# Moving a block's state stores, its last degree sums and its first late masks between nodes of a graph recurrence

## Chip, core and metric

One core of a Trainium2 chip runs the whole program: four graph layers over 64 graphs of 256 nodes with 256 features, in float32. The metric is device time in microseconds (us) of one execution, lower is better. The kernel is written for the five engines of the core: TensorE (PE, matrix products), VectorE (DVE), ScalarE (ACT), GpSimd (POOL) and SyncE (SP, which here only issues DMAs).

## What is computed

Layer 0 is a recurrence over the 256 nodes of a graph: node i's parent vector is the sum of the states of the other nodes weighted by column i of the adjacency, divided by row i's degree; a gated cell makes the new state of node i from it, and later nodes see that new state. All 64 graphs advance together. Layers 1 to 3 (a normalized graph convolution and two attention layers) follow, each with residual and layer norm; the change doesn't touch them.

```python
d = jnp.sum(adj, axis=-1)
dinv = jnp.where(d != 0, 1.0 / jnp.where(d != 0, d, 1.0), 0.0)
norm_adjT = jnp.swapaxes(adj, 1, 2) * dinv[:, :, None]

def step(h, i):
    x = jnp.take(h_e, i, axis=1)
    row = jnp.take(norm_adjT, i, axis=1)
    x_par = jnp.einsum('bj,bjd->bd', row, h)
    iou = x @ W_ioux.T + b_ioux + x_par @ W_iouh.T + b_iouh
    r, z = jnp.split(iou, 2, axis=1)
    r, z = (jax.nn.sigmoid(r), jax.nn.sigmoid(z))
    hc = jnp.tanh(x @ W_coux.T + b_coux + x_par * r @ W_couh.T + b_couh)
    h_new = z * x_par + (1.0 - z) * hc
    h = jax.lax.dynamic_update_slice(h, h_new[:, None, :], (0, i, 0))
    return (h, None)
h_out, _ = jax.lax.scan(step, h_e, jnp.arange(n))
```

## The kernel before

`_recurrence` walks the nodes one at a time (the loop at line 768). Nodes are counted in blocks of T = 32 (block k, node i inside it) and in octets of U = 8 (p = n % 8). The loop is traced under a manual schedule, so every engine works its instructions strictly in the order in which the code states them; SP's one queue carries nearly all DMAs, in the order of the code too.

A node's chain is short and serial: transpose of the parent vector (`flip`, 618), products with the gate weights (`h_part`, 611), a sigmoid on ACT (835), transpose (837), the product `rT` on DVE (839), products again, tanh on ACT (872), and on DVE `zcc` (874) and the next parent vector `xp` (877). The rest of the node's work is laid beside this chain:

- A state's share in later sums. DVE pushes a new state into the sums of the near nodes (`push`, 636), POOL into the farther ones of the octet and the next (`push_far`, 674 and 678). POOL also makes `ready` (816), the finished sum of the next node times its inverse degree; DVE reads it at 864.
- The late side, for states that are up to some 48 nodes old. They lie in `Hw`, a ring of 64 rows a half of the graphs (partition = 64 x half + node % 64); `into_ring` (667) writes each new state there with two DMAs, in the nodes with p of 4 to 7. In the nodes with p of 0 to 3, PE multiplies ring rows by `An`, the masked adjacency of the block (527). The results are copied to `lb`, sent to DRAM (`Lb<-lb`, 507) and read back in another layout (`late_sb<-Lb`, 513) about a node later. POOL adds `late_sb` to the sums (887) at p = 6 and 7, that is at nodes 14, 15, 22, 23 and so on of the block, before any node of the next octet.
- The early side, for older states. They are stored in DRAM (`Hd`) by `flush` (646), read back by `early_load`, multiplied on PE (424), and come to POOL as `early_sb` (829) at p = 3 and 4.
- Tables of the next block, made during this one. `degrees` (292) is a generator of 14 steps. Four times it loads four rows of adjacency a graph at a time (`rows`, one buffer, two DMAs of 256 KB) and sums them on DVE in two halves (304); then it inverts the sums and copies the result into `dinv`. The loop takes a step of it at the nodes of a list (911). `late_load` (460) queues loads of `raw`, the adjacency that `An` is cut from, and POOL multiplies it with the window mask in four pieces (`cut`, 485) at fixed nodes. The first piece also forces any load of `raw` that is still in the list of waiting loads.

`flush` copies 16 ring rows of both halves with two DMAs. A row of the ring is 32 KB on one partition, so a DMA moves 512 KB from 16 neighbouring partitions (480 KB where 15 rows are stored). At i = 16 a block stores 31 rows: the second half of the block before, and the first half of its own but for the newest state, which `state_out` (652) stores straight from its tile.

Within a node, the order on SP is: ring writes, loads from the list (p < 4), steps placed by `at_step`, the reads for the next octets, the stores of `flush`, then a step of `degrees`.

Of the kernel before, what the change touches and what calls it, by code (L numbers as in the profile page):

```python
# [70 lines left out]
def _recurrence(tc, ident, Hd, x, adj, W_ioux, b_ioux, W_iouh, b_iouh, W_coux, b_coux, W_couh, b_couh, wide, then):  # L71
# [21 lines left out]
    T = 32  # L93
# [7 lines left out]
    HB = B // 2  # L101
    FAR = (2, 4, 4, 4, 4, 4, 3, 4)

    with ExitStack() as ctx:
# [14 lines left out]
        def ring(lo, hi):  # L119

            while lo < hi:
                end = min(hi, (lo // W + 1) * W)
                yield lo, end, lo % W
                lo = end
# [125 lines left out]
        def next_load(n):  # L250
            if loads:
                loads.pop(0)[1](n)
# [10 lines left out]
        def load_later(out, in_, rank):  # L263

            begun = []

            def f(n):
                with nc.allow_non_contiguous_dma(reason="bias vector across partitions"):
                    nc.sync.dma_start(out, in_)
                begun.append(n)  # L270

            loads.append((rank, f))
            loads.sort(key=lambda e: e[0])
            return begun
# [5 lines left out]
        def at_step(n, f):  # L280
            transfers.setdefault(n, []).append(f)
# [10 lines left out]
        def degrees(k):  # L292

            R = 4
            HT = T // 2
            deg = work.tile([P, HT], F32, tag="deg", name=f"deg_{k}")
            for r in range(0, HT, R):
                rows = stream.tile([P, R, N], F32, tag="rows", name=f"rows_{k}_{r}", bufs=1)
                for h in range(2):
                    at = k * T + h * HT + r  # L300
                    nc.sync.dma_start(rows[h * B:(h + 1) * B], adj[:, at:at + R, :])
                yield
                for e in range(0, R, 2):
                    nc.vector.tensor_reduce(
                        deg[:, r + e:r + e + 2], rows[:, e:e + 2, :], AX.X, ALU.add
                    )
                    yield
            zero = work.tile([P, HT], F32, tag="deg0", name=f"deg0_{k}")
            inverse(deg, zero)
            yield  # L310
            dinv_from(deg, k)
# [148 lines left out]
        def late_load(k, n=None):  # L460


            An = blk.tile([P, HB, U, T // U], F32, tag="An", name=f"An_{k}")
            raw = stream.tile([P, HB, T], F32, tag="raw", name=f"raw_{k}", bufs=1)
            first, last = k * T - W + T // 2, k * T + T // 2
            if first < 0:
                nc.gpsimd.memset(raw, 0.0)
            begun = []
            for lo, hi, at in ring(max(first, 0), last):
                for g in range(2):  # L470
                    to = raw[g * W + at:g * W + at + hi - lo]
                    of = adj[g * HB:(g + 1) * HB, lo:hi, k * T:(k + 1) * T].rearrange(
                        "b j i -> j b i"
                    )
                    if n is None:
                        nc.scalar.dma_start(to, of)
                    else:
                        begun.append(load_later(to, of, 1.5))

            def cut(lo):  # L480
                while not all(begun):
                    next_load(now)
                part = raw[:, lo:lo + HB // 4].rearrange("p b (s u) -> p b s u", u=U)
                take = window[k % 2].rearrange("p (s u) -> p s u", u=U).unsqueeze(1)
                nc.gpsimd.tensor_mul(
                    An[:, lo:lo + HB // 4].rearrange("p b u s -> p b s u"), part,
                    take.to_broadcast(list(part.shape)),
                )

            for e in range(4):  # L490
                if n is None:
                    cut(e * HB // 4)
                else:
                    at_step(n + (12, 15, 20, 23)[e], lambda e=e: cut(e * HB // 4))
            return An

        def late(first):
# [43 lines left out]
        def load_S(k, n=None):  # L541

            S = blk.tile([P, LAG + T, T], F32, tag="S", name=f"S_{k}")
            lag = min(LAG, k * T)
            to, of = S[0:B, LAG - lag:], adj[:, k * T - lag:(k + 1) * T, k * T:(k + 1) * T]
            begun = [0] if n is None else load_later(to, of, 1.5)
            if n is None:
                nc.sync.dma_start(to, of)
            if not lag:
                nc.gpsimd.memset(S[:, LAG - 1], 0.0)  # L550

            def double():
                while not begun:
                    next_load(now)
                nc.sync.dma_start(S[B:, LAG - lag:], S[0:B, LAG - lag:])

            return S, double

        def chain_S(k):

            Sd = blk.tile([P, T], F32, tag="Sd", name=f"Sd_{k}")
            flat = tables[k]["S"].rearrange("p j i -> p (j i)")
            first = (LAG - 1) * T
            nc.vector.tensor_mul(
                Sd, flat[:, first:first + (T - 1) * (T + 1) + 1:T + 1],
                dinv[:, k * T:(k + 1) * T],
            )
            return Sd

        def load_x(a):  # L570

            xq = stream.tile([P, U // 2, D], F32, tag="xq", name=f"xq_{a}")
            for h in range(2):
                at = a * U + h * U // 2
                nc.sync.dma_start(xq[h * B:(h + 1) * B], x[:, at:at + U // 2, :])
            return xq
# [63 lines left out]
        def flush(lo, hi):  # L640

            for lo in range(max(lo, 0), hi, T // 2):
                end = min(hi, lo + T // 2)
                for g in range(2):
                    at = g * W + lo % W
                    nc.sync.dma_start(
                        Hd[lo:end, g * HB:(g + 1) * HB, :], Hw[at:at + end - lo]
                    )

        def state_out(n, hs):  # L650
            for o in range(2):
                nc.sync.dma_start(Hd[n][:, o * P:(o + 1) * P], hs[o * B:(o + 1) * B])
# [72 lines left out]

        tables[0]["Sd"] = chain_S(0)
        tables[0]["An"] = late_load(0)
        xq = {a: load_x(a) for a in range(2)}
        for a in range(3):
# [38 lines left out]
        for now in range(N):  # L768
            n = now
            k, i = divmod(n, T)  # L770
# [124 lines left out]
                sums_in(n // U + 3)  # L895
            if p == 2 and n // U + 2 < N // U:
                xq[n // U + 2] = load_x(n // U + 2)
            if i == T // 2:
                state_out(n - 1, hs)
                flush(n - T, n - 1)  # L900
            if n == N - U + 3:
                assert all(j >= N - U for j, _ in ring_in)
                flush(N - T // 2, N - U)
# [4 lines left out]
            if k + 1 < NB:  # L908
                if i == 0:
                    background = degrees(k + 1)  # L910
                if i in (0, 2, 3, 8, 10, 11, 12, 15, 16, 17, 19, 20, 22, 24):
                    next(background, None)
                if i == 0:
                    tables[k + 1]["S"], double = load_S(k + 1, n)
                    at_step(n + 19, double)
                    tables[k + 1]["An"] = late_load(k + 1, n)
                if i == 28:
                    tables[k + 1]["Sd"] = chain_S(k + 1)
# [554 lines left out]
def kernel(ctx: ExitStack, tc: tile.TileContext, ins, out):  # L1473
# [14 lines left out]
    def load_layers(load):  # L1488
        weights.extend(
            _load_layers(nc, wide, load, ins["L1_gnn_W"], ins["L1_gnn_b"], l2, l3)  # L1490
        )

    _recurrence(
        tc, ident, Hd, x, adj,
        *(ins["L0_gnn_" + n] for n in (
# [44 lines left out]
```

## Time and profile before

| what | us |
|---|---|
| time, median of 3 runs (lowest, highest) | 3335.34 (3333.89, 3336.39) |
| the profiled execution: time, span of its instructions | 3328.66, 3326.6 |
| the recurrence, node 0's `rT` to node 255's | 139.9 to 1486.5 |
| `L304`, sums of degree rows on DVE, 56 of them, each | 0.68 |
| `L485`, mask pieces on POOL, 32 of them, each | 0.74 |
| `L887`, adds of the late side on POOL, 60 of them, each | 1.27 |

Every node has one `rT` product (L839), so in the timeline of DVE the starts of L839 divide the recurrence into nodes. The interval called 19 runs from node 19's `rT` to node 20's, and holds the end of node 19, where the side work of that node stands. Some of them, in us:

| block | 10 | 11 | 13 | 16 | 18 | 19 | 20 | 21 | 22 | 23 |
|---|---|---|---|---|---|---|---|---|---|---|
| 0 | 5.0 | 5.2 | 4.8 | 5.7 | 6.0 | 5.2 | 4.8 | 4.5 | 4.9 | 8.1 |
| 1 | 5.0 | 5.2 | 4.8 | 5.6 | 4.8 | 14.6 | 6.9 | 4.5 | 5.5 | 12.7 |
| 2 | 5.0 | 5.2 | 4.8 | 5.4 | 4.8 | 12.0 | 7.2 | 4.5 | 4.5 | 4.4 |
| 3 | 5.0 | 5.2 | 4.6 | 9.9 | 4.8 | 10.5 | 6.8 | 4.6 | 4.6 | 4.5 |
| 4 | 5.0 | 5.1 | 7.9 | 11.0 | 4.8 | 11.5 | 7.7 | 4.6 | 4.6 | 4.5 |
| 5 | 5.0 | 5.1 | 4.4 | 6.0 | 5.9 | 8.4 | 6.0 | 4.5 | 4.8 | 4.4 |
| 6 | 5.0 | 5.2 | 4.4 | 6.1 | 4.8 | 8.7 | 6.7 | 4.4 | 4.4 | 4.6 |
| 7 | 4.8 | 4.8 | 4.7 | 5.6 | 4.8 | 4.8 | 4.4 | 4.4 | 4.4 | 4.4 |

Block 0 has nothing to store from a block before it, and block 7 has no next block whose degrees it would sum.

### The profile page before, as it was taken

What the parts mean: (1) busy time and instruction counts of PE and PEld (TensorE: products, weight loads), DVE (VectorE), ACT (ScalarE), POOL (GpSimd) and SP (SyncE); (2) the same over time, 40 slices, a digit from 0 to 9 for tenths busy, and PEclk for the clock granted to TensorE, in tenths of its full rate; (3) what the DMA queues carried; (4) which work ended last, traced back from release to release, by engine and by line L of the source; (5) the groups of instructions that cost most, each with busy time, mean ns of one, the idle gap of its engine ahead of it and who ended that gap; (6) DMA issues with size and microseconds to landing.
All of it is one profiled execution on the core that took longest, in us unless ns stands there. A gap on an engine that the chain in (4) does not pass through costs nothing.

```text
span 3326.6 us, 80047 instructions
## 1 busy us (share of the span) xinstructions
PE 3083.6 (93%) x28332; PEld 2279.5 (69%) x28332; DVE 2625.7 (79%) x7511; ACT 1834.3 (55%) x4690; POOL 1924.5 (58%) x2230
## 2 busy tenths in 40 slices
PE   5799979898989898986999999999999999999997
PEld 4565646565555555554888888888888888888885
DVE  3476757787767787864888888888888888888886
ACT  0154535454545454543666666666666666666664
POOL 2376757776767788853555555555555555555543
PEclk8899989999999999997999999999999999999998
DMA  9864556686866675334233333333333333333310
GB/s 293 249 169 126 156 149 157 167 186 165 199 169 159 160 175 151 103 73 99 61 77 77 77 77 77 79 79 77 82 79 80 77 79 77 78 80 78 77 45 20
DMA packets 806730, 385.73 MB, mean 116 GB/s; under 512 B 525260, under 2 KB 774232, under 8 KB 802648
## 3 DMA queue, kind: packets, MB, share of 16 engines
q1 hardware_dynamic: 788632, 363.66, 45.2%
q10 hardware_dynamic: 17696, 16.91, 1.5%
q8 instruction: 227, 3.72, 0.5%
q14 instruction: 175, 1.43, 0.1%
HBM read 261.75 MB, written 99.61 MB: 109 GB/s over the span
## 4 chain that ended last, share of the span: by engine, by line
PE 79%; DVE 8%; DMA 7%; issue 2%; ACT 1%; SPq 1%; POOL 1%; DVEq 0%; ACTq 0%; POOLq 0%
PE mm L1017 14%; PE rc L611 7%; PE rc L603 4%; PE s L1243 4%; PE mm_3v L1017 4%; PE mm_2f L1017 4%; PE mm_2v L1017 3%; PE mm_3f L1017 3%; PE mm_t L1017 3%; PE late L527 3%; PE mm_g L1017 3%; PE mm_2w L1017 3%; PE mm_2s L1017 3%; PE o L1278 3%; DVE ACC L636 3%; PE z_ps L611 3%
## 5 line engine op out<-in xcount | busy, mean ns | idle before, releaser
L1255 POOL TENSOR_TENSOR p3s<-p 128x256 f32<-128x256 f32 x512 | 359.0, 733 | 267.8 <-ACT p L1253 267.7
L1017 PE MATMUL mm<-xT,weights 128*128 128x256 f32 x2048 | 483.6, 384 | 2.7 <-ACT xT L1133 2.7
L636 DVE SCALAR_TENSOR_TENSOR ACC<-keep,S,ACC 128x128 f32<-128x128 f32 x1712 | 478.9, 343 | 5.6
L1017 PEld LDWEIGHTS mm<-xT,weights 128*128 128x128 f32 x2048 | 385.8, 191 | 80.0 <-ACT xT L1133 28.8
L678 POOL TENSOR_TENSOR ACC<-ACC,far 128x384 f32<-128x384 f32 (+1 forms) x313 | 372.4, 1190 | 24.5
L1252 DVE TENSOR_TENSOR p<-s,neg 128x512 f32<-128x512 f32 x512 | 317.7, 683 | 83.5 <-PE s L1243 83.5
L973 ACT ACTIVATE y<-y,shift,rstd 128x256 f32<-128x256 f32 x512 | 279.7, 596 | 158.3 <-DVE shift L971 158.1
L1253 ACT ACTIVATE p<-p 128x512 f32<-128x512 f32 x512 | 307.2, 629 | 3.3 <-DVE p L1252 3.0
L674 POOL TENSOR_TENSOR far<-hs,S 128x384 f32<-128x384 f32 (+1 forms) x313 | 304.8, 974 | 4.7
L816 POOL TENSOR_TENSOR ready<-ACC,dinv 128x128 f32<-128x128 f32 x255 | 102.3, 401 | 340.5 <-DVE ACC L636 340.1
L603 PE MATMUL rc<-WxT,xqT 128*64 128x256 f32 x2048 | 276.6, 392 | 0.2 <-issue 0.2
L965 POOL TENSOR_TENSOR rstd<-rstd,mhalf 128x2 f32<-128x2 f32 x256 | 173.8, 696 | 134.2 <-DVE rstd L964 132.4
L611 PE MATMUL rc<-WhT,rT 128*64 128x128 f32 x2048 | 174.7, 293 | 58.2 <-DVE rT L839 57.6
L1292 DVE RECIPROCAL rT<-o 128x256 f32<-128x256 f32 x128 | 223.7, 1748 | 0.0
L961 DVE BATCH_NORM_STATS2 st<-y 128x6 f32<-128x256 f32 x512 | 209.6, 409 | 12.8 <-POOL y L1154 9.9
L611 PEld LDWEIGHTS rc<-WhT,rT 128*64 128x64 f32 x2048 | 110.7, 140 | 155.8 <-DVE rT L839 136.9
L1154 POOL TENSOR_TENSOR y<-y,g 128x512 f32<-128x512 f32 x64 | 81.2, 1268 | 216.8 <-ACT g L1151 197.2
L835 ACT ACTIVATE rs<-rc 128x128 f32<-128x128 f32 x256 | 71.1, 278 | 244.6 <-PE rc L611 244.6
L611 PE MATMUL rc<-WhT,xpT 128*64 128x128 f32 x2048 | 169.1, 286 | 39.6 <-ACT xpT L620 36.3
L1165 ACT ACTIVATE qk<-mm,weights 128x256 f32<-128x256 f32 x256 | 107.4, 470 | 164.7 <-PE mm L1017 162.8
L611 PEld LDWEIGHTS rc<-WhT,xpT 128*64 128x64 f32 x2048 | 107.0, 136 | 120.7 <-ACT xpT L620 110.1
L839 DVE TENSOR_TENSOR rT<-rT_ps,xpT 128x128 f32<-128x128 f32 x256 | 74.2, 290 | 141.6 <-PE rT_ps L837 139.1
(168 smaller groups left out, 7337.2 us busy)
## 6 DMA issues: line engine op xcount, KB each, us to landing
xX<-in_x_dram ACTq DMA_DIRECT2D x16, 1024.0 KB
Us<-xu SPq DMA_DIRECT2D x64, 256.0 KB
xq<-in_x_dram SPq DMA_DIRECT2D x64, 256.0 KB
ACC<-Us SPq DMA_DIRECT2D x32, 512.0 KB
Es<-eu SPq DMA_DIRECT2D x64, 256.0 KB
early_sb<-Es SPq DMA_DIRECT2D x32, 512.0 KB
xin<-in_x_dram SPq DMA_DIRECT2D x64, 256.0 KB
ad<-in_adj_dram SPq DMA_DIRECT2D x64, 256.0 KB
```

The lines of the kernel that those rows point to most:

```text
L603: nc.tensor.matmul(G[o * B:(o + 1) * B], xqT[a, i // 2][:, i % 2, kc, h * B:(h + 1) * B], WxT[:, kc, o, gates], start=False, stop=False, s ...
L611: nc.tensor.matmul(G[o * B:(o + 1) * B], hT[:, kc * B:(kc + 1) * B], WhT[:, kc, o, g], start=False, stop=(kc == 1), skip_group_check=True,)
L636: nc.vector.scalar_tensor_tensor(acc[:, 0, :], keep[:, j % 2, :], s, acc[:, 0, :], ALU.mult, ALU.add)
L674: nc.gpsimd.tensor_mul(tmp[:, 0:count, :], hs.unsqueeze(1).to_broadcast(shape), s.unsqueeze(2).to_broadcast(shape),)
L678: nc.gpsimd.tensor_add(acc, acc, tmp[:, 0:count, :])
L961: nc.vector.bn_stats(st, y[:, c, :])
L973: nc.scalar.activation(y[:, c, :], y[:, c, :], AF.Identity, bias=shift[:, c:c + 1], scale=rstd[:, c:c + 1],)
L1017: nc.tensor.matmul(pm[:, c, :], lhsT[:, k, c * P:(c + 1) * P], rhs[:, k, :], start=(k == 0), stop=(k == 1),)
L1252: nc.vector.tensor_add(p, s_ps[i], self.neg3)
L1253: nc.scalar.activation(p, p, AF.Exp, scale=ISQ)
L1255: nc.gpsimd.tensor_add(both, p[:, 0, :], p[:, 1, :])
L1292: nc.vector.reciprocal(rT, o_ps[:, 1, :])
```

## The change

Three things move; nothing is added or taken away. `flush` for the second half of the block before is called at i = 10 instead of i = 16, so two of the four large stores of a block stand six nodes sooner (blocks 1 to 7). The list of `degrees` has (20, 21, 23) for (19, 20, 22): the two sums of the last four rows and the inversion stand a node later; the load of those rows stays at 17 and the copy into `dinv` at 24. The first two mask pieces stand at nodes 15 and 18 for 12 and 15, the third at 21 for 20, the fourth stays at 23. The forcing of waiting `raw` loads stays at node 12, now as a step of its own.

```diff
@@ late_load
-            def cut(lo):
+            def begin():
                 while not all(begun):
                     next_load(now)
+
+            def cut(lo):
                 part = raw[:, lo:lo + HB // 4].rearrange("p b (s u) -> p b s u", u=U)
...
+            if n is not None:
+                at_step(n + 12, begin)
             for e in range(4):
                 if n is None:
                     cut(e * HB // 4)
                 else:
-                    at_step(n + (12, 15, 20, 23)[e], lambda e=e: cut(e * HB // 4))
+                    at_step(n + (15, 18, 21, 23)[e], lambda e=e: cut(e * HB // 4))
...
+            if i == 10:
+                flush(n - 26, n - 10)
             if i == T // 2:
                 state_out(n - 1, hs)
-                flush(n - T, n - 1)
+                flush(n - T // 2, n - 1)
...
-                if i in (0, 2, 3, 8, 10, 11, 12, 15, 16, 17, 19, 20, 22, 24):
+                if i in (0, 2, 3, 8, 10, 11, 12, 15, 16, 17, 20, 21, 23, 24):
                     next(background, None)
```

## The prediction

> **What bounds the kernel now.** The change lies in layer 0, so I read the waits of VectorE first, then the timelines of VectorE, SyncE and GpSimd around the largest, then windows of busy time for the clock and the DMA share. Columns of the waits: us in total, times, longest.
>
> ```profile
> DVE rT L839 <- PE rT_ps L837: 139.1, 181, 8.6
> DVE deg L304 <- DMA rows<-in_adj_dram: 34.1, 6, 9.3
> ```
>
> The first is the node's own chain. The second is side work that stops it: six times, once a block in blocks 1 to 6, DVE waits for the last four degree rows at node 19 (9.3, 6.7, 5.2, 6.2, 3.1 and 3.5 us, from the timeline). Block 4:
>
> ```profile
> 947.60 0.35 DVE L877 SCALAR_TENSOR_TENSOR xp<-zcc,Sd,keep 128x128 f32<-128x128 f32 x1
> 954.18 0.69 DVE L304 TENSOR_REDUCE deg<-rows 128x2 f32<-128x512 f32 x1 [6.23 <-DMA rows<-in_adj_dram]
> 954.78 0.28 DVE L657 TENSOR_TENSOR keep<-zcc,keep 128x128 f32<-128x128 f32 x1
> ```
>
> Behind the sum stand that node's pushes and the next `rT`; PE and POOL stop with them. Why the rows are late is seen on SP, in block 2 and then in block 0, which stores only two pieces:
>
> ```profile
> 587.87 10.09 SPq L646 DMA_DIRECT2D Hd<-Hw  x4
> 598.06 2.85 SPq L316 DMA_DIRECT2D ACC<-Us  x1
> 601.01 2.84 SPq L301 DMA_DIRECT2D rows<-in_adj_dram  x2
> ```
> ```profile
> 218.46 1.03 SPq L646 DMA_DIRECT2D Hd<-Hw  x2
> 219.61 4.08 SPq L269 DMA_DIRECT2D xA<-in_adj_dram  x1
> 223.74 4.76 SPq L269 DMA_DIRECT2D xX<-in_x_dram  x1
> 228.59 0.45 SPq L316 DMA_DIRECT2D ACC<-Us  x1
> 229.13 1.55 SPq L301 DMA_DIRECT2D rows<-in_adj_dram  x2
> ```
>
> Four stores hold SP for 10 us, and the rows, issued at 601, land at 610.2. Two stores cost as well: the next two issues stick for 4.08 and 4.76 us. The DMA records say the same: the stores' 32 KB packets run 219.6 to 229.4 with two stores and 590.0 to 604.2 with four, the first two done at 598.8. So two cost about 9.3 us and four about 14.
>
> After the stall, node 20 is slow too. The windows of block 4 (PE, PEld, DVE, ACT, POOL busy, granted clock, DMA share, GB/s) show why:
>
> ```profile
> 941.20:946.00 4.80, 4.74 (x76) 2.91 (x76) 4.39 (x17) 2.79 (x10) 2.67 (x4) 1.00 0.69 198
> 957.50:965.00 7.50, 7.50 (x62) 4.47 (x58) 4.36 (x15) 2.19 (x8) 5.57 (x6) 0.64 0.34 105
> ```
>
> The granted clock falls to 0.64 once PE has stood still, and interval 20 takes 7.7 us.
>
> **What the skill says.** The Trainium skill, "TensorE: Matmul & The Clock Gate", Part 1, has an idle PE fall to half clock after an idle window of about 3.4 us and come back after a busy one; the 0.64 agrees. "SBUF — State Buffer", Door 1, gives 16 neighbouring partitions only 4 of 16 DMA ports, 104 GB/s measured; here 960 KB took 9.8 us, 100 GB/s, which agrees. "DMA: Bandwidth & Descriptors", Queues, rings and completion order, has each DMA engine start an SP ring's descriptors in order: a large store delays whatever is issued behind it.
>
> **The change, part by part.** *Sums a node later, half of the stores gone from node 16.* Intervals 19 + 20 + 21 sum to 26.0, 23.7, 21.9, 23.8, 18.9 and 19.8 us in blocks 1 to 6, 134.1 in all. Without the wait I take 5.1 + 5.2 + 5.0 = 15.3: 5.1 is what nodes of that place take without a sum; intervals 10 and 11, which have one, take 5.0 and 5.2; 21 gets a sum and a mask on its 4.5. Six times 15.3 is 91.8; removed: 42.3 us. Is the cover there? DVE now reaches the sum some 5.1 us later, and the rows land 14.2 - 9.3 = 4.9, say 4.7 us, sooner. Together 9.8 us against waits of at most 9.3, so all six go, block 1's barely. A miss costs what is late plus about 2 us of slow clock.
>
> *The new stores at node 10.* Two SP issues of about 0.5 us in each of blocks 1 to 7; nobody reads their data before node 18. They cost through the ring: 9.3 us of DMA. Queued behind them on SP: `raw`, the late side's `Lb<-lb` and `late_sb<-Lb`, the ring writes, the rows of node 12. In blocks 1, 2 and 5 the DMA share falls to 0.04, 0.02 and 0.07 after node 10 (windows 365 to 373, 557 to 563, 1071 to 1077), and POOL takes `late_sb` 8 to 9 us after its issue, about 3 us of which is the transfer: hidden. Block 6 may lose 0.5. Blocks 3 and 4 are full there (share 1.06 from 725 to 735, 1.04 from 900 to 910). Block 4, SP then POOL:
>
> ```profile
> 903.69 5.42 SPq L507 DMA_DIRECT2D Lb<-lb  x2
> 909.22 2.34 SPq L667 DMA_DIRECT2D Hw<-hs  x4
> 912.61 0.34 SPq L513 DMA_DIRECT2D late_sb<-Lb  x1
> ```
> ```profile
> 911.23 0.73 POOL L485 TENSOR_TENSOR An<-raw,window 128x256 f32<-128x256 f32 x1 [5.78 <-issue]
> 916.84 1.27 POOL L887 TENSOR_TENSOR ACC<-ACC,late_sb 128x512 f32<-128x512 f32 x1
> ```
>
> `late_sb` lands at about 915.4; with 9 us of stores ahead, 924.4, against a use at about 913.7 (the mask's stall gone). That is up to 10.7 us of POOL, of which I take 7.5 on the path, since POOL's 5.78 at the mask cost interval 13 only 3.1. Block 3 lands at 739.7 and is used at 743.0: up to 5.7 late, I take 3.5. Bounds for both together: 0 if the stores overlap the loads, 18 with the clock.
>
> *Masks.* 21 pieces of 0.74 us on POOL move from nodes 12, 15 and 20 to 15, 18 and 21; PE needs them all only from node 24, and the fourth piece stays. Block 4's 5.78 us wait at node 12 goes: 3.1 us saved. The rest I take at nothing, hidden in POOL's idle time before `ready`; bounds 3 us either way. The inversion (five DVE operations, under 1 us) a node later is nothing: the copies to `dinv` stay at 24.
>
> *What is late next.* Node 22 uses the late side too. Block 1: `late_sb<-Lb` goes out at 432.47, lands at 435.5, is used at 437.92. The queue empties 4.7 us sooner (430.8), but the node comes 10.7 sooner (427.2): 3.6 us of wait, and behind it SP's ring writes and the stores of `xu` that ACT awaits at node 23 (7.6 us now). I give back 5. Block 2 gives back 0.5; blocks 3 to 6 have 7 to 12 us between issue and use, enough.
>
> Sum: 42.3 + 3.1 - 5 - 0.5 - 3.5 - 7.5 - 0.5 = 28.4 us of the profiled 3328.66. That execution is 6.7 us under the median of the runs; I take the same saving from the median: 3335.3 - 28 = 3307.
>
> **Rivals.** *All of it stays (0.25).* The stores overlap the loads in blocks 3 and 4, and only block 1 gives back: 45.4 - 5.5 = 40, 3295. For it: POOL idles in most nodes. Against it: the full DMA share there. *The late round trip takes over (0.15).* At node 22 every block waits for `late_sb` as block 1 does, so a block gains only the 4.7 us by which the queue empties: 28, less 11 at node 14, 17 us, 3318. Against it: the 7 to 12 us of room in blocks 3 to 6. *Slower (0.08).* At node 14 every one of the seven blocks waits the way block 4 would, because the stores at node 10 hold the ring ahead of `Lb<-lb`: 9 us each, 63 against 45, 3353. It decides from 45 / 7 = 6.4 us a block; against it stand the idle DMA windows of blocks 1, 2 and 5. The likeliest case has 0.52.
>
> **How the numbers follow.** A measurement of this kernel can tell about 0.2%, 6.7 us. The likeliest case runs from the bounds at node 14 (0 to 18) and the masks: 3296 to 3318. Reaching into its neighbours, the range is 3293 to 3323. Faster: 0.50 + 0.25 + 0.11 = 0.86; the same 0.02 + 0.03 + 0.01 = 0.06; slower 0.08.
>
> **What would show it.** Right: no wait of L304 for `rows`, intervals 19 and 20 near 5.2 with the clock at 1.00, and a new wait of L887 for `late_sb` in blocks 4, 3 (node 14) and 1 (node 22). Wrong: L304 still waits at node 20 (two stores cost what four did), or blocks 1, 2 and 5 stall between nodes 11 and 16.

## The result and the profile after

The changed kernel takes 3310.38 us (median of 4 runs, 3302.49 to 3314.75), the kernel before 3334.61 beside it (3329.19 to 3336.39). The ratio is 0.9927, with a 95% interval of 0.9905 to 0.995: some 24 us saved, where 28 were predicted. The profiled execution of after takes 3314.75 us (span 3313.0), 4.4 above its median, while that of before was below its own. So the two traces show only part of it: the recurrence goes from 1346.5 to 1331.8 us, 14.7 less. Lines below the edits have moved: `rT` is now L843, the stores L650, the late side's products L531 and its add L891.

The waits of VectorE after (us in total, times, longest):

```profile
DVE rT L843 <- PE rT_ps L841: 140.5, 172, 9.5
DVE deg L721 <- DMA rows<-in_adj_dram: 13.9, 1, 13.9
```

The group of 34.1 us at L304 is gone; L721 is the one wait for rows that is left, ahead of the recurrence, and it was there before. VectorE's timeline in block 4, at node 20, where the sum now stands:

```profile
950.70 0.35 DVE L881 SCALAR_TENSOR_TENSOR xp<-zcc,Sd,keep 128x128 f32<-128x128 f32 x1
950.97 0.68 DVE L304 TENSOR_REDUCE deg<-rows 128x2 f32<-128x512 f32 x1
951.56 0.29 DVE L661 TENSOR_TENSOR keep<-zcc,keep 128x128 f32<-128x128 f32 x1
```

No bracket behind the sum: it starts as soon as `xp` is done. SyncE's timeline in block 2 at node 16:

```profile
588.55 1.04 SPq L650 DMA_DIRECT2D Hd<-Hw  x2
589.68 4.25 SPq L316 DMA_DIRECT2D ACC<-Us  x1
594.03 5.46 SPq L301 DMA_DIRECT2D rows<-in_adj_dram  x2
```

Two stores still hold the issues behind them (4.25 and 5.46 us), but the issue of the rows begins 5.5 us after the stores, not 13.1, and ends 10.9 us after them, not 16.0. The windows of block 4 (PE, PEld, DVE, ACT, POOL busy, granted clock, DMA share, GB/s), the intervals 18, 20 and 14:

```profile
939.10:943.90 4.80, 4.75 (x82) 2.91 (x88) 4.40 (x16) 2.78 (x10) 3.37 (x5) 1.00 0.57 154
948.90:954.10 5.20, 5.20 (x66) 3.27 (x63) 4.46 (x16) 2.29 (x9) 4.02 (x6) 1.00 0.56 152
905.10:917.60 12.50, 5.17 (x66) 2.92 (x64) 3.15 (x12) 2.72 (x10) 2.73 (x4) 0.88 0.56 147
```

Interval 20 takes 5.2 us at a clock of 1.00, where it took 7.7 at 0.64 before, and is now like its undisturbed neighbour. The third line is new: interval 14 takes 12.5 us, 4.6 before. SyncE and then GpSimd show why:

```profile
895.30 1.04 SPq L650 DMA_DIRECT2D Hd<-Hw  x2
896.39 2.84 SPq L269 DMA_DIRECT2D raw<-in_adj_dram  x1
899.33 7.38 SPq L511 DMA_DIRECT2D Lb<-lb  x2
906.81 2.33 SPq L671 DMA_DIRECT2D Hw<-hs  x4
909.31 0.34 SPq L517 DMA_DIRECT2D late_sb<-Lb  x1
909.75 1.18 SPq L301 DMA_DIRECT2D rows<-in_adj_dram  x2
```
```profile
915.22 1.26 POOL L891 TENSOR_TENSOR ACC<-ACC,late_sb 128x512 f32<-128x512 f32 x1 [9.31 <-DMA rows<-in_adj_dram]
```

Behind the new stores `Lb<-lb` sticks for 7.38 us, `late_sb` is read back late, and POOL stands for 9.31 us. The releaser named is `rows`, but the instruction reads `late_sb`, issued just ahead of it: by the trace's semaphore events that load lands at 915.09, 0.13 us ahead of the add. In the second measurement of this kernel (e5) the same wait is put down to it:

```profile
910.97 1.26 POOL L891 TENSOR_TENSOR ACC<-ACC,late_sb 128x512 f32<-128x512 f32 x1 [9.65 <-DMA late_sb<-Lb]
```

By intervals of nodes, summed over the eight blocks, against the profile of before (us; from the starts of `rT` in VectorE's timeline; the runs e1 to e12 are described below). The last column tells how far the execution that was profiled lies from the median of its kernel; that of before lies 6.0 us under it:

| kernel | 19-21 | 12-15 | 16 | 22-24 | 8 | rest | recurrence | execution - median |
|---|---|---|---|---|---|---|---|---|
| predicted | -42.3 | +8.4 | 0 | +5.5 | 0 | 0 | -28.4 | |
| after | -46.7 | +6.7 | +4.0 | +12.6 | +1.8 | +6.9 | -14.7 | +4.4 |
| after again (e5) | -42.6 | +8.2 | +4.6 | +10.2 | +4.6 | +0.9 | -14.1 | +3.9 |
| e1 | -44.3 | +5.2 | +2.9 | +9.7 | +4.1 | +6.7 | -15.7 | +8.1 |
| e2 | -28.5 | -1.3 | -1.3 | +22.7 | +3.8 | +7.8 | +3.2 | +5.0 |
| e3 | -30.4 | +6.5 | +3.2 | -0.4 | +2.2 | +9.8 | -9.1 | +7.9 |
| e4 | +4.1 | -0.2 | +1.8 | +1.1 | -1.1 | -0.5 | +5.2 | -2.4 |
| e6 | -45.4 | -1.6 | +64.3 | +5.9 | +1.1 | +5.2 | +29.5 | +1.1 |
| e7 | -45.6 | -1.2 | -0.8 | +15.0 | +57.9 | +3.3 | +28.6 | +8.3 |
| e8 | -47.4 | +8.5 | +30.9 | -0.4 | +6.3 | +24.6 | +22.5 | +13.3 |
| e9 | -47.3 | +7.4 | +1.7 | +2.5 | +0.7 | +0.5 | -34.5 | -6.8 |
| e10 | -44.9 | -1.6 | +3.2 | +18.9 | +3.5 | -2.3 | -23.2 | -1.9 |
| e11 | -47.3 | +2.8 | +3.2 | +10.1 | +9.4 | +18.5 | -3.3 | +1.7 |
| e12 | -46.2 | +6.9 | +5.0 | +3.4 | +1.8 | +0.6 | -28.5 | +2.0 |

Between two executions of one kernel (after and e5) "rest" moves by 6 us, "19-21" by 4, "8" and "22-24" by 2 to 3, so only larger entries are read. For the time of a kernel the ratios of the medians count, not the column "recurrence".

### The profile page after: what moved, and what is told of

Its sections match the earlier page's. It is cut to its first block, busy times and chain, and to the rows that moved or that the text cites. A ratio compares the mean times of both kernels' runs of the same rounds, so it can differ in the third digit from the quotient of the medians.

```text
span 3313.0 us, 80062 instructions
## 1 busy us (share of the span) xinstructions
PE 3077.3 (93%) x28332; PEld 2275.4 (69%) x28332; DVE 2630.6 (79%) x7511; ACT 1834.0 (55%) x4690; POOL 1925.8 (58%) x2230
## 4 chain that ended last, share of the span: by engine, by line
PE 79%; DMA 8%; DVE 7%; issue 2%; SPq 2%; ACT 2%; POOL 1%; DVEq 0%; ACTq 0%; POOLq 0%
PE mm L1023 14%; PE rc L615 7%; PE rc L607 4%; PE s L1249 4%; PE mm_3v L1023 4%; PE mm_2f L1023 4%; PE late L531 3%; PE mm_2v L1023 3%; PE mm_3f L1023 3%; PE mm_t L1023 3%; PE mm_g L1023 3%; PE mm_2w L1023 3%; PE mm_2s L1023 3%; PE o L1284 3%; DVE ACC L640 3%; PE z_ps L615 2%
## 5 line engine op out<-in xcount | busy, mean ns | idle before, releaser
L967 DVE BATCH_NORM_STATS2 st<-y 128x6 f32<-128x256 f32 x512 | 209.6, 409 | 12.6 <-POOL y L1160 9.7
L531 PE MATMUL late<-Hw,An 64*32 64x256 f32 x3840 | 165.4, 396 | 25.6 <-DMA A<-in_adj_dram 9.9
```

The costliest lines, as they stand in the source:

```text
L531: nc.tensor.matmul(pb[g][q * T:(q + 1) * T, e, :], An[rows, b].rearrange("p u s -> p (u s)"), Hw[rows, b, :], start=True, stop=True,)
```

## The experiments

**e1_inv22: the inversion back at node 22.** One thing in the trace of after that no step had foreseen was interval 23, 1.1 to 1.5 us longer in blocks 0 and 2 to 6 (3.3 in block 1). VectorE and then GpSimd there, block 2 of after:

```profile
622.01 0.35 DVE L881 SCALAR_TENSOR_TENSOR xp<-zcc,Sd,keep 128x128 f32<-128x128 f32 x1
622.28 0.89 DVE L227 TENSOR_SCALAR deg<-deg 128x16 f32<-128x16 f32 x1
623.20 0.65 DVE L228 TENSOR_TENSOR deg<-deg,deg 128x16 f32<-128x16 f32 x1
623.89 0.25 DVE L229 RECIPROCAL deg<-deg 128x16 f32<-128x16 f32 x1
```
```profile
621.86 1.27 POOL L891 TENSOR_TENSOR ACC<-ACC,late_sb 128x512 f32<-128x512 f32 x1
623.10 0.74 POOL L487 TENSOR_TENSOR An<-raw,window 128x256 f32<-128x256 f32 x1
```

The two small operations of the inversion end when the POOL instructions beside them end (623.17 against 623.13, 623.85 against 623.84), 0.89 and 0.65 us long on 128 x 16 numbers. Node 23 has POOL's second late add and the fourth mask in just this place.

```diff
-                if i in (0, 2, 3, 8, 10, 11, 12, 15, 16, 17, 20, 21, 23, 24):
+                if i in (0, 2, 3, 8, 10, 11, 12, 15, 16, 17, 20, 21, 22, 24):
```

> The changed kernel with the inversion of the degrees back at node 22 (the sums stay at 20 and 21). Port theory: at node 23 the inversion's DVE operations L227 and L228 (0.17 us each before, up to 0.94 and 0.66 us now) wait for POOL's adds and the mask that stand in the same node, and interval 23 is 1.1 to 1.5 us longer in blocks 0 to 6. Then L227 and L228 go back to 0.17 us in nearly all blocks, interval 23 is about 1.2 us shorter in seven blocks, and the time is about 8 us under the changed kernel, some 3302 us. Rival (interval 23 is longer because the ring writes and stores of the DMA queue lag behind the faster nodes): interval 23 stays, and the time is that of the changed kernel within 3 us.

Measured: 3303.51 us, ratio 0.9894 (0.988 to 0.9908). Interval 23 is back at 4.4 us in blocks 2 to 6. In blocks 0 and 1 it stays 2.0 and 1.9 us longer than before, so what was seen there is not the inversion's. The same lines of block 2:

```profile
619.88 0.43 DVE L227 TENSOR_SCALAR deg<-deg 128x16 f32<-128x16 f32 x1
620.34 0.17 DVE L228 TENSOR_TENSOR deg<-deg,deg 128x16 f32<-128x16 f32 x1
```

So the later inversion cost 6.8 us in interval 23 of blocks 2 to 6, against after and against its second measurement alike. Not all of that is gained in e1: the same blocks are 0.8 us slower there at interval 22 and 2.1 at 24, so that 3.9 us are left. The medians of the two kernels differ by 6.9 us (3310.38 - 3303.51), and their intervals of the ratio overlap (0.9908 and 0.9905). The Trainium skill, "SBUF — State Buffer", "Who interferes with whom", has a VectorE instruction with two inputs in SBUF contend with a GpSimd instruction that reads SBUF, and one in a two-port mode shut a GpSimd instruction out, or be shut out by it, for the whole instruction. The ends of the instructions agree with that; in which mode `L227` runs, no trace here shows.

**e2_sums_only, e3_stores_only, e4_masks_only: each part of the change alone, on the kernel before.**

```diff
 e2: -(..., 17, 19, 20, 22, 24)
     +(..., 17, 20, 21, 23, 24)
 e3: +            if i == 10:
     +                flush(n - 26, n - 10)
...
     -                flush(n - T, n - 1)
     +                flush(n - T // 2, n - 1)
 e4: -n + (12, 15, 20, 23)[e]
     +n + (15, 18, 21, 23)[e]      (with the forced loads at n + 12)
```

> The kernel before with the moved degree sums alone (20, 21, 23); all four stores at node 16, masks as before. Cover theory: the waits of 9.3, 6.7, 5.2, 6.2, 3.1 and 3.5 us shrink by the 5.1 us of a node, so about 7 us of waiting for rows is left, in blocks 1, 2 and 4; nothing is lost at node 14; the inversion at 23 costs some 8 us; gain 22 to 30 us, about 3308. Rival (the stores are the cause, and nothing helps but moving them): more than 20 us of waiting for rows is left at node 20, gain under 10 us, 3325 or more.

> The kernel before with the stores of the older half at node 10 alone; sums at 19 and 20, masks as before. Cover theory: the rows land about 5 us sooner, so about 7 us of waiting is left at node 19; block 4 loses 8 us or more at nodes 13 and 14, block 3 about 4 at node 16; no cost at node 23; gain 15 to 25 us, about 3315. Rival (two stores at node 16 hold the rows as long as four): over 20 us of waiting left at node 19 and no gain.

> The kernel before with the moved masks alone. Block 4's wait of POOL for raw at node 12 (5.8 us, 3.1 us of interval 13) goes, nothing else changes: 3 us of gain, 3331, which is no more than a measurement of this kernel can tell. Rival (masks in nodes 18 and 21 collide with other work on POOL and DVE): intervals 15, 18 and 21 are longer by 0.3 us or more in seven blocks, and the gain is gone.

Measured, with 3336.38 us before: e2 3330.49, ratio 0.9985 (0.9976 to 0.9994); e3 3309.04, ratio 0.9911 (0.9896 to 0.9925); e4 3335.11, ratio 0.9991 (0.9982 to 1.0). The waits of VectorE for the rows, e2 and then e3:

```profile
DVE deg L304 <- DMA rows<-in_adj_dram: 13.5, 4, 5.5
```
```profile
DVE deg L304 <- DMA rows<-in_adj_dram: 10.8, 4, 5.3
```

Each alone leaves a part of the 34.1 us, the sums 40%, the stores 32%. But the time divides otherwise: the stores alone are worth as much as the whole change, the sums with the inversion almost nothing. In e2 what intervals 19 to 21 gave, 28.5 us, is given back in 22 to 24 (+22.7) and elsewhere. Some 3.5 us of this are the inversion, which e2 moves along with the sums (interval 23 of blocks 3, 4 and 6, where `L228` took 0.66 us); no run moves the sums without it and leaves the stores. For the rest, four stores still hold the queue, and the nodes only reach the next customers of it sooner (POOL waits for `late_sb` at node 22 of blocks 1, 2 and 5, PE for ring rows at node 24 of blocks 2 and 4). A consumer that comes later takes its own wait away, not the cause of it. e4 moves the mask's stall of block 4 on: interval 13 falls by 3.3 us, 14 and 16 rise by 1.6 and 2.1; the 3 us of gain that were expected don't show.

**e5_again: the changed kernel once more**, beside the next three.

> The changed kernel once more, beside the next three, so that they can be compared on one chip: some 3308 to 3312 us, ratio 0.992 to 0.993. Port theory: slower than the version with the inversion at 22 by 5 us or more, as that one was 3303.5; rival (the 7 us between them were between chips): ratio at or under 0.990.

3309.62 us, ratio 0.9921 (0.9907 to 0.9935), as the first time. One wait of L304 for rows is left in this trace, 0.83 us at node 20 of block 1.

**e6_store13, e7_store6, e8_actq: the stores elsewhere**, on e1. e6 has the first pair at node 13, e7 at node 6; e8 leaves the nodes and issues all large stores from ScalarE's queue.

```diff
-            if i == 10:
-                flush(n - 26, n - 10)
+            if i == 13:
+                flush(n - 29, n - 13)
```
```diff
-                    nc.sync.dma_start(
+                    nc.scalar.dma_start(
                         Hd[lo:end, g * HB:(g + 1) * HB, :], Hw[at:at + end - lo]
```

> The changed kernel with the inversion at node 22 and the older half's stores at node 13, behind the late round trip of nodes 11 and 12 on SP's queue. Ring theory: what stands behind the stores is late, so block 4's wait of 7 to 9 us for late_sb at node 14 goes (interval 14 near 4.6 us), while the ring writes of nodes 13 to 15 come behind them and PE waits 2 to 4 us more for them at node 16 in blocks 3 and 4; time 3298 to 3305. Rival (the DMA engines are full there, and any place between 8 and 16 loses the same): block 4 still loses 6 us or more in intervals 12 to 15.

> The changed kernel with the inversion at node 22 and the older half's stores at node 6, before the reads of blocks 3 and 4 fill the queue. Ring theory: late_sb at node 14 is on time in blocks 3 and 4 (some 7 us of gain there), but the stores now stand ahead of the degree rows of node 8, which DVE wants at node 10, and of early_sb for node 11: waits of 2 to 5 us there in blocks 2 to 4; time 3298 to 3308. Rival (no effect beyond node 8): intervals 10 and 11 stay at 5.0 and 5.2 and the time falls to 3296.

> The changed kernel with the inversion at node 22 and all stores of flush issued on ACT's queue in place of SP's, at the same nodes 10 and 16. Ring theory: the stores delay others because these stand behind them in the same ring and because SP sticks in their issue; then SP's issues after node 16 take about 0.6 us each, block 4's wait at node 14 shrinks to under 3 us and late_sb is on time at node 22 of block 1: 3285 to 3296. Rival (a store's descriptors occupy the DMA engines from whichever ring): the waits at nodes 14, 16 and 22 stay within 2 us of what they were and the time is 3300 to 3306. Third (ACT sticks in the issue as SP did): ACT stands still for over 3 us at nodes 16 and 17 and the time is over 3310.

Measured, with 3333.32 us before: e6 3357.68, ratio 1.0059 (1.0043 to 1.0075); e7 3350.16, 1.0045 (1.0027 to 1.0063); e8 3341.09, 1.002 (1.0008 to 1.0032). All three are slower than the kernel before. The expected times all failed but e8's above 3310 us. What was expected at node 14 came: interval 14 of block 4 is 5.5, 4.6 and 4.6 us in e6, e7 and e8, 12.5 in after. But the waits that e7 was to have at nodes 10 and 11 didn't come, and the wait for the ring writes, 2 to 4 us in two blocks of e6 by the expectation, is far larger. Three nodes later or four sooner cost about 50 us. The table shows where: e6 loses 64.3 us in interval 16, e7 57.9 in interval 8, in each of blocks 1 to 7. SyncE and then PE in block 4 of e6:

```profile
927.61 5.31 SPq L650 DMA_DIRECT2D Hd<-Hw  x2
933.02 5.60 SPq L671 DMA_DIRECT2D Hw<-hs  x4
```
```profile
947.27 1.11 PE L531 MATMUL late<-Hw,An 64*32 64x256 f32 x16 [13.28 <-DMA Hw<-hs]
```

Nodes 4 to 7 of an octet issue the ring writes, and the products of the next node 0 read them. Node 13 lies inside this stretch (so does 6): the ring writes of nodes 14 and 15 wait behind the stores, and PE waits at node 16 for them, 13.28 us here. At node 10 the next ring write is two nodes off, and the products that need it six. The stores cost 8 to 9 us a block at either wrong place (64.3 / 7, 57.9 / 7), as the slower rival of the prediction had it, but by the ring writes and not by `Lb<-lb`.

ScalarE in block 4 of e8, node 10 (ACTq are the DMAs that it issues):

```profile
900.03 0.31 ACTq L650 DMA_DIRECT2D Hd<-Hw  x1
900.40 0.60 ACT L256 COPY lb<-late 128x512 f32<-128x512 f32 x1
908.82 0.31 ACTq L650 DMA_DIRECT2D Hd<-Hw  x1
909.18 0.27 ACT L624 COPY xpT<-xpT_ps 128x128 f32<-128x128 f32 x1 [8.18 <-DMA Hs<-Hd]
```

The second store goes out 8 us after the first, and `xpT`, which is on the node's chain, comes after it. The store's own issue takes 0.31 us. What it waits for, by the trace's semaphore events, is the completion semaphore that it takes over from a load of `Hs`: SP had issued this load at 893.51, and it lands at 908.80. So the releaser named is right, and ScalarE stands for another DMA to land. Six of the 15 pairs of stores at nodes 10 and 16 wait in this way, in blocks 1 to 4; in blocks 5 and 6 the second store of node 10 took 4.58 us to issue, as stores do on SP. On SP such holds delay DMAs, on ScalarE they delay the recurrence. Nor was SP set free: behind the stores of node 16 an issue of `rows` still took 3.8 to 4.5 us in blocks 1, 2, 5 and 6, where 0.6 was expected. The Trainium skill, "DMA: Bandwidth & Descriptors", "Issuing engines are not separate DMA queues", has DMAs of all issuers run on the same 16 engines, which agrees. What stores on a second queue would be worth with semaphores of their own is not shown.

**e9_late18, e10_all18, e11_store8: order against earliness.** From e6 and e7 a new theory: what counts is only what stands behind the stores on SP's queue. Node 18 lies like node 10, and the rows of node 17 go ahead of it. On e1:

```diff
 e9, second pair:      e10, all four:
             if i == T // 2:
                 state_out(n - 1, hs)
-                flush(n - T // 2, n - 1)
+            if i == 18:
+                flush(n - 18, n - 3)      (e10: n - 34, and nothing at 10)
```
```diff
 e11
-            if i == 10:
-                flush(n - 26, n - 10)
+            if i == 8:
+                flush(n - 24, n - 8)
```

> The kernel of e1_inv22 with the second pair of stores at node 18 instead of 16 (the newest state is still stored at 16). Place theory: what counts is only what stands behind the stores on the queue; node 18 has, like node 10, the first ring write two nodes behind it, and the rows of node 17 now go ahead, so it costs nothing: 3300 to 3308, interval 24 near 5.6. Round-trip theory: the late side's read back at node 22 now stands behind the stores, as at node 14 of block 4; blocks 1 and 2 lose 3 to 8 us at interval 22: 3310 to 3323.

> The kernel of e1_inv22 with all four large stores at node 18, none at 10. If the order behind the rows is what the whole gain comes from, the waits of the sums for rows are gone here too, though no store is sooner: 42 us less than before, less what the 14 us of stores do to the late side's read back at node 22 and the ring writes before node 24: 3308 to 3325. If a queue that is held for 14 us must stop something whatever stands behind it, the loss comes back there in every block (about 6 us in interval 22 or 24): 3330 to 3350.

> The kernel of e1_inv22 with the first pair of stores at node 8 instead of 10, just ahead of the rows that are loaded at node 8 and summed at nodes 10 and 11. Order theory: the wait of the sums comes back there, about 3 us and 2 us of slow clock in blocks 1 to 6, 30 us in all: 3325 to 3338. If the six ring-write-free nodes are all that counts (8 is the first of them), node 14 of block 4 gains instead: 3295 to 3303.

Measured, with 3331.09 us before: e9 3296.53, ratio 0.9891 (0.9873 to 0.991); e10 3308.05, 0.9931 (0.9909 to 0.9952); e11 3322.83, 0.9967 (0.9953 to 0.998). SyncE in block 2 of e9:

```profile
577.48 1.14 SPq L301 DMA_DIRECT2D rows<-in_adj_dram  x2
578.72 1.27 SPq L579 DMA_DIRECT2D xq<-in_x_dram  x2
580.04 1.02 SPq L650 DMA_DIRECT2D Hd<-Hw  x2
```

The rows go first and are issued in 1.14 us instead of 5.46. Of block 1's wait for `late_sb` at node 22, 3.99 us in after, 1.56 are left, and its interval 22 is as in the kernel before, against the round-trip theory. The time is under the expected 3300 to 3308, but the ratio is that of e1: on top of sums that stand later, the later second pair shows no gain. e10 stores nothing sooner than the kernel before, and everything two nodes later, and yet has the whole gain of intervals 19 to 21: no L304 wait is left. (Its sums stand at the later nodes; e12 takes that away.) It pays in 22 to 24 (+18.9); GpSimd in block 2 at node 22:

```profile
619.01 1.26 POOL L891 TENSOR_TENSOR ACC<-ACC,late_sb 128x512 f32<-128x512 f32 x1 [4.76 <-DMA late_sb<-Lb]
```

This is what the round-trip rival described, with four stores (10.6 to 13.2 us in the DMA records of blocks 1 to 6) instead of two. And e10, without stores at node 10, has interval 14 of block 4 at 5.7 us (after 12.5) and interval 16 of block 3 at 9.0 (after 13.9): the early stores are the cause of both losses. (A part only moves: interval 16 of block 4 is 2.5 us longer in e10 than before.) e11 sets the old fault up at another place; SyncE and VectorE in block 4:

```profile
880.22 0.92 SPq L650 DMA_DIRECT2D Hd<-Hw  x2
881.18 8.98 SPq L301 DMA_DIRECT2D rows<-in_adj_dram  x2
```
```profile
894.62 0.69 DVE L304 TENSOR_REDUCE deg<-rows 128x2 f32<-128x512 f32 x1 [4.89 <-DMA rows<-in_adj_dram]
```

The wait of the sum is back, at node 10, in blocks 3 to 6 (9.5 us in all). Intervals 10 and 11 are 14.5 us longer than before (e1: 1.0). The expected 30 us were too many, since blocks 1 and 2 have no such wait, and the time just misses the expected 3325 to 3338; the ratio is 0.7% over e1's, and what makes up the rest of it was not placed.

**e12_order_only: the kernel before with only the stores moved, to nodes 10 and 18.** Sums, inversion and masks stay at their old nodes.

```diff
+            if i == 10:
+                flush(n - 26, n - 10)
             if i == T // 2:
                 state_out(n - 1, hs)
-                flush(n - T, n - 1)
+            if i == 18:
+                flush(n - 18, n - 3)
```

> The kernel before with the first pair of stores at node 10 and the second at node 18; sums, inversion and masks stand where the kernel before has them. Order theory: the rows of node 17 go ahead of all stores, so the sums at 19 and 20 don't wait even at their old nodes (e3_stores_only left 10.8 us of such waits at node 19), the inversion stays at 22, and only the mask at node 12 of block 4 costs some 3 to 8 us against e9_late18: ratio 0.989 to 0.992, about 3295 to 3305. If the sums needed their later node all the same: waits of L304 of 10 us or more, ratio 0.993 or above.

Measured: 3296.86 us against 3338.56, ratio 0.9879 (0.9852 to 0.9906). No wait of L304 is left although the sums are at node 19 again. It differs from e3 in the second pair alone, at node 18 for 16, and e3 had 10.8 us of these waits: the order on the queue takes them away. GpSimd's waits for `raw` at the masks (the other one, of 9.0 us, lies ahead of the recurrence and was there before):

```profile
POOL An L485 <- DMA raw<-in_adj_dram: 18.8, 2, 9.8
```

The wait of 9.8 us is in block 4, whose interval 13 is 5.5 us longer than before. It was expected to cost 3 to 8 us against e9, and costs nothing: e9 loses 7.8 us at interval 14 of this block, e12 0.3, and intervals 12 to 15 sum to the same (+7.4 and +6.9). So the place of the masks decides at which node this block is stalled, and not for how long.

e12 and e9 can't be told apart; both, like e1, beat the kernel before by 1.1 to 1.2%. Against the changed kernel the ratios are 0.3 to 0.5% lower, but most of the intervals overlap; only e12 and the second measurement of after are just apart (0.9906 and 0.9907).

## Why the prediction was right, and where not

- *The four stores hold the rows, and splitting them frees the sums.* Right: no wait of L304 (0.83 us in e5), intervals 19 and 20 near 5 us, the clock at 1.00. Intervals 19 to 21 gave 46.7 us for the 42.3 predicted.
- *The cover, 5.1 us of a later node and 4.7 of earlier rows.* The second half fits e3: taking 4.7 from each of the six waits leaves 8.6 us, measured 10.8. The first half fits e2 in three blocks (8.0 us left where 6.9 were to be) and fails in block 3: 5.49 us for 0.1. There the four stores took 15.7 us in the DMA records (13.0 before), and node 19 began 10.0 us after the first of them was issued (12.2 before), together some 5 us. The later sums were not needed either: with the second pair of stores behind the rows (e12) they don't wait at their old nodes.
- *Block 4, node 14.* As predicted: +7.8 us for 7.5, by `late_sb`; the mask's interval 13 falls by 3.3 (3.1). e10 shows that the stores cause most of it. But the 3.1 us are no saving of the masks: with the masks left alone, e3 and e12 lose 6.5 and 6.9 us in intervals 12 to 15, the changed kernel 6.7 and 8.2. And the 9.3 us of stores ahead of `Lb<-lb` were too many: at node 10 the pair took 5.8 to 7.5 us in the DMA records, 7.0 in this block.
- *Block 3, node 14, 3.5 us.* The size was right and the place wrong. POOL waited 1.75 us for `late_sb` at node 14, but interval 14 lost 0.3; interval 16 lost 4.1, where PE's wait for the ring went from 2.87 to 6.33 us. The ring writes, which also stand behind the stores, were named and not followed to their consumer. This is the mechanism that decides e6 and e7.
- *Block 1, node 22.* The wait of 3.99 us for `late_sb` is there (3.6 predicted), and the wait of `xu` at node 23 went from 7.60 to 10.52 us. What was taken back in this block's intervals 22 and 23 is 4.3 us (+1.0 and +3.3; 5 predicted), 3.5 in e5.
- *"The inversion a node later is nothing".* This step failed. It costs 6.8 us in interval 23, 3.9 with its neighbours (e1): its duration was read at node 22, and what POOL does beside it at node 23 wasn't looked at. The trace of before has a sign of it even at node 22: in block 1 `L227` took 1.20 us, in the others 0.17 to 0.23, and ended at 440.45, when the POOL instruction beside it did (440.42).
- *The sum.* 28 us predicted and 24 measured by the ratio, but the terms don't add up so well. Intervals 22 to 24 gave back 12.6 and 10.2 us for 5.5 predicted, interval 16 lost 4.0 and 4.6 for nothing; against it stands the gain in 19 to 21, 4.4 us over the prediction in the first trace, 0.3 in the second. The two traces of after show 14.7 and 14.1 us; that the medians show 24 fits with where the executions lie in the last column of the table (6.0 under for before, 4.4 and 3.9 over for after). So the mechanism was right, and that the number came so near is in part luck. *All of it stays* falls with block 4; *the late round trip takes over* happened in e10 and not here, where only block 1 waits at node 22; *slower* needs stores ahead of something that every block waits for, which node 10 avoids and nodes 6 and 13 don't.

Whether the 0.3% between e1 and the changed kernel is all the inversion is not settled beyond the intervals of blocks 2 to 6: the intervals of the ratio overlap or touch (0.9908 for e1; 0.9905 and 0.9907 for after).

## What to carry to other kernels

A large transfer on an in-order DMA queue is placed by what stands behind it: list every issue between it and the time that it is done, follow each to its consumer, and put the transfer right after the urgent ones. Moving the consumer that waits helped little here, since the next one on the queue inherited the wait. And an operation that is moved is priced again at its new place, by what the other engines do there.

## What the hardware showed unexpectedly

- The same pair of 512 KB stores took 5.7 to 7.5 us where it was issued at node 10 and 9.9 to 10.8 us at nodes 6 and 13 (DMA records of 32 KB; e9, e7 and e6). The first is 140 to 184 GB/s, above the 104 GB/s that the prediction takes as agreed. Why it differs isn't shown: at nodes 6 and 13 ring writes stand behind the stores, but the second pair, at node 16 of after without any, took 8.2 to 10.1 us for 960 KB.
- A VectorE operation on 128 x 16 numbers took 0.17 us alone and up to 0.94 us beside POOL instructions (after), so even tiny side work on VectorE can make an interval 1.1 to 1.5 us longer.
- ScalarE stood for 8.18 us ahead of a store, of which the issue takes 0.31 us, because the store took over the completion semaphore of a load that SP had issued and that had not landed.
